# A two-layer decoder on one core: layer 0's contexts loaded turned, their norm moved into weights and evictions; layer 1's normed rows stored turned

## The chip, the cores and the metric

One core of a Trainium2 chip runs the whole program in one launch. The metric is the device time in microseconds (us) of one execution. Its engines are TensorE (PE: matrix products and, through products with an identity, transposes), VectorE (DVE), ScalarE (ACT), GpSimd (POOL) and SyncE (SP, which here only issues DMAs). Each engine works through its own queue in order; an instruction that waits holds up all behind it on that queue. PE writes its results to PSUM, and DVE or ACT must read ("evict") them before the PSUM bank can be used again.

## What is computed

A decoder of two layers on x (32 batches of 100 tokens, 256 wide, float32). Each layer has self-attention, cross-attention to contexts of 361 rows of 192, and a feed-forward part with experts. Two parts matter here.

Layer 0's cross-attention normalizes the contexts, then makes keys and values from them:

```
xn = layernorm(ctx, ln_x_g, ln_x_b)          # (32, 361, 192): mean and variance per row
ln = layernorm(layernorm(x), ln_l_g, ln_l_b) # (32, 100, 256)
q  = ln @ Wq.T
kv = concat([xn @ Wkv.T, ln @ Wlkv.T])       # 461 rows, 256 keys and 256 values
```

Keys and queries are normalized per head of 64, the scores masked, exponentials taken, and the weighted values projected and added to x.

Layer 1's feed-forward part takes the normed rows xn = layernorm(x). All rows go through one shared expert, silu(xn @ w1.T) @ w2.T, and each row also through two of eight experts with weights from a softmax.

## The kernel before

The program is unrolled and its stages follow each other. In each stage the program order of PE, DVE, ACT and POOL is the one written (`in_order`, L227); SP's order is written by hand only in the last two stages, elsewhere the framework sets it. PSUM has eight banks: two `sc` tiles of two banks each, and four `mm` tiles of one bank (`mm_tile`). A new `mm` tile takes a bank that has been read out.

**Layer 0's self-attention** (to about 290 us) is `heads_attention`: round s makes the scores of batch s+1, turns the weights of batch s (`turn_weights`, L390 on PE and L395 on ACT), makes values and sums. `fill(s, part)` is called at four places in a round and puts in work for the next stage: the first context loads, norms and turns.

**Layer 0's cross-attention** (about 290 to 760 us) works on one batch a round, at several depths at once. The loop over n (from L922) writes the order out. For a context, round n does: `context(n+6)`, the load of its rows (L552, L555); `context_normed(n+6, 0)`, mean and variance on DVE (L161, L162, L170) and the factor by a power on POOL (L174); `context_normed(n+5, 1)`, the centred and scaled rows `cn` on DVE (L183); `context_turned(n+4, 0)` and `(n+4, 1)`: transposes on PE (L574 for columns 0 to 127, L577 for the last 64, made twice, into both halves of the partitions) and evictions with gain and bias into cT by ACT (L583) and DVE (L587). Then `keys_values(n+3)`: eight products on PE (L720, L725; four tiles, two of 512 columns and two of 256), evicted by ACT (keys and values of the first 128 rows, keys of the last 105) and DVE (the rest), L733 to L737.

The rest of a round, in order: the square of the keys on ACT (`squares(n+2)`, L762), `keys_turned(n+1)` (PE L798, L806; kT by ACT L801; the queries qT by DVE L809), POOL's `divided(n, 1)` (L865) after DVE's reciprocal (L864), `output(n-1)` (PE L223 with x_wo, DVE L909), the sums of squares (L768) and the root on POOL (L772), `own_keys_values(n+3)` (PE L223 with x_wl into two tiles; keys by ACT L751, values by DVE L757), `turn_weights(n)` (PE L874, ACT L877), `keys_normed(n+2)` (L779, L780 on DVE, L782 on POOL), the keys and values above, `scores(n+1)` (L832 into `sc` tiles), `sums(n)` (L888), `exponentials(n+1)` (per head DVE L851 subtracts and masks, ACT L855 takes the exponential; after two heads ACT copies the sums out, L898), and `divided(n+1, 0)`. Every four rounds `latents_turned` adds eight transposes.

**Layer 1's cross-attention** ends at about 2835 us. Among its rounds `gating(g, part)` normalizes the rows of four batches (part 1, ACT L192), stores them to DRAM (`xn_dram`, L1589), turns them for the gate (part 2: transposes L210, evictions L131 and L133 into gT, one buffer, which lnT of the next group uses two units later) and sorts them to the experts.

**The shared expert** (about 2835 to 3025 us) loads blocks of 512 normed rows (`rows_of`, L2064), turns them (`rows_turned`: eight transposes L2077, evictions L131 and L133) and then makes, for every 256 rows and 128 hidden columns, L223 with the first weights, Silu on ACT (L2104) and the second product L2112. The routed experts follow to the end.

Of the kernel before, what the change touches and what calls it, by code (L numbers as in the profile page):

```python
# [10 lines left out]
F32 = mybir.dt.float32  # L11
# [7 lines left out]
P = 128  # L19
B, T, D = 32, 100, 256  # L20
S2, DC = 361, 192
G = 4
# [44 lines left out]
def kernel(ctx: ExitStack, tc: tile.TileContext, io: dict, out: bass.AP):  # L67
# [82 lines left out]
    def stats(src, n, np_=T, twice=False, tag="", half=None, got=None, shift=False):  # L150
# [7 lines left out]
        va = small.tile([P, G], F32, tag="va", name="va")  # L158
        rs = norms.tile([P, G], F32, tag="rs" + tag, name="rs")
        for i in range(n // 2 if half == 1 else 0, n // 2 if half == 0 else n):  # L160
# [374 lines left out]
    cbs, cns, cTs, lns, lnTs = {}, {}, {}, {}, {}  # L535

# [13 lines left out]
    def context(b):  # L550
        cb = cbuf[b % 2]
        nc.sync.dma_start(  # L552
            cb[:, 0:2, :], io["ctx"][b, 0:256].rearrange("(c p) d -> p c d", p=P)
        )
        nc.sync.dma_start(cb[:105, 2, :], io["ctx"][b, 256:S2])  # L555
        cbs[b] = cb

    def context_normed(b, part):
        if part == 0:
            cns[b] = stats(cbs[b], 3, P, tag="c")  # L560
        else:
            cn = early_ctx.tile([P, 3, DC], F32, tag="cn", name="cn")
            centered(cn, cbs.pop(b), 3, cns[b], P)
            cns[b] = cn

    def context_turned(b, c):

        if c == 0:
            cTs[b] = early_ctx.tile([P, 2, S2], F32, tag="cT", name="cT")
        cn, cT = cns[b], cTs[b]  # L570
        pt = mm_tile()
        for k, (k0, kn) in enumerate(CCH):
            if c == 0:
                nc.tensor.transpose(pt[:, k0 : k0 + kn], cn[:kn, k, 0:P], ident[:kn, :kn])  # L574
                continue
            for e in range(2):
                nc.tensor.matmul(  # L577
                    pt[64 * e : 64 * e + 64, k0 : k0 + kn], cn[:kn, k, P:DC],
                    ident[:kn, :kn], start=True, stop=True, tile_position=(0, 64 * e),
                )  # L580
        gain, bias = col("x0_xg", c), col("x0_xb", c)
        if c == 0:
            return lambda: nc.scalar.activation(  # L583
                cT[:, 0, :], pt[:, :S2], AF.Identity, bias=bias, scale=gain
            )
        cns.pop(b)
        return lambda: nc.vector.tensor_scalar(  # L587
            cT[:, 1, :], pt[:, :S2], gain, bias, ALU.mult, ALU.add
        )

    with tc.tile_pool(name="a0", bufs=2) as pool:
# [19 lines left out]
        def fill(s, part):  # L611
            for f, *args in {
                (B - 5, 0): ((context, 0), (context, 1)),
                (B - 3, 0): ((context_normed, 0, 0),),
                (B - 3, 2): ((latents, 0, 0),),
                (B - 2, 0): ((latents, 0, 1),),
                (B - 2, 2): ((context_normed, 0, 1),),
                (B - 1, 0): ((context_normed, 1, 0),),
                (B - 1, 1): ((latents, 0, 2),),
                (B - 1, 3): ((context_normed, 1, 1),),  # L620
            }.get((s, part), ()):
                f(*args)
            if s < B:
                return
            if part == 0:
                lnTs[0] = latents_turned(lns.pop(0))
            elif part < 3:
                context_turned(0, part - 1)()
            else:
                latents(1, 0)  # L630
                context(2)
                context_normed(2, 0)

# [53 lines left out]
    with tc.tile_pool(name="x0", bufs=2) as pool, tc.tile_pool(name="x0p", bufs=1) as fixed:  # L687
# [7 lines left out]
        for n in range(3):  # L695
# [15 lines left out]
        def keys_values(b, part):  # L711
# [18 lines left out]
            kvs.pop(b), cTs.pop(b)  # L730
            kb, vb = kbs[b], vbs[b]
            for n, copy in enumerate((nc.scalar.copy, nc.vector.tensor_copy)):
                copy(kb[:, n, :], ps[n][:, :D])  # L733
                copy(vb[:, n, :], ps[n][:, D:])
            kn = CCH[2][1]
            nc.scalar.copy(kb[:kn, 2, :], ps[2][:kn, :D])
            nc.vector.tensor_copy(vb[:kn, 2, :], ps[3][:kn, :D])  # L737

        def own_keys_values(b):

            lnT = lnTs[b // G]
            kb = kbs[b] = kbuf[b % 3]
            vb = vbs[b] = pool.tile([P, 4, D], F32, tag="vb", name="vb", bufs=4)
# [12 lines left out]
            )  # L756
            nc.vector.tensor_copy(vb[:T, 3, :], ps[:T, :D])  # L757

# [29 lines left out]
        def keys_turned(b, c):  # L788
# [20 lines left out]
            nc.vector.tensor_scalar(  # L809
                qT.rearrange("p c t -> p (c t)"), pt[:, : 2 * T], gains, None, ALU.mult  # L810
            )
# [106 lines left out]
        with in_order():  # L918


            for n in range(-3, B + 1):
                at(n + 6, context)  # L922
                at(n + 2, mask, 0)
                at(n + 2, squares)
# [8 lines left out]
                for k in range(4):  # L933
                    at(n, turn_weights, k)
                at(n + 5, context_normed, 1)
                if 0 <= n + 4 < B:
                    context_turned(n + 4, 0)()
                g = (n + 4) // G + 1
# [3 lines left out]
                if (n + 5) % G >= 1 and g + 1 < NG:  # L942
                    latents(g + 1, (n + 5) % G - 1)
                at(n + 6, context_normed, 0)
                at(n + 2, keys_normed)
# [590 lines left out]
    x_dram = dram.tile([NTOK, D], F32, name="x_dram")  # L1536
    xn_dram = dram.tile([NTOK, D], F32, name="xn_dram")
    acc_dram = dram.tile([NTOK + P, D], F32, name="acc_dram")
# [15 lines left out]
    )  # L1554
    gated = {}

    def largest(val, which, got=None):
# [24 lines left out]
    def gating(pool, g, part):  # L1582
# [4 lines left out]
        elif part == 1:  # L1587
            scaled(xs[g], xs[g], G, gated[g])
            nc.sync.dma_start(  # L1589
                xn_dram[g * GT : (g + 1) * GT, :].rearrange("(i t) d -> t i d", t=T), xs[g]  # L1590
            )
# [86 lines left out]
    with tc.tile_pool(name="x1", bufs=2) as pool, tc.tile_pool(name="x1p", bufs=1) as fixed:  # L1678
# [297 lines left out]
        with in_order():  # L1976
            for part in range(2):
                normed(0, part)
            lns[0] = turned(lns[0])
            qTs[0] = query_tile()  # L1980
            for m in range(8):
                queries(qTs[0], lns[0], m)
            keys(0, 0)
            keys(0, 1)
            for n in range(-2, NU):
                turn_of(n)
            for n in range(NU, NU + 4):
                sends(n)
            for part in range(3):
                finish(NG - 1, part)  # L1990
# [63 lines left out]
    with tc.tile_pool(name="f1s", bufs=2, side="right") as pool, in_order(SP):  # L2054
        xns_, xTs_, hTs, accs, held = {}, {}, {}, {}, {}
        pace = pool.tile([1, 1], F32, name="pace", bufs=1)
        NB = -(-NCH // 4)
        NHB = -(-NCH // 2)

        def rows_of(n):  # L2060

            cn = min(4, NCH - 4 * n)
            xn = pool.tile([P, 4, D], F32, tag="xn", name="xn")
            nc.sync.dma_start(  # L2064
                xn[:, :cn, :],
                xn_dram[512 * n : 512 * n + cn * P, :].rearrange("(c p) d -> p c d", p=P),
            )
            xns_[n] = xn

        def rows_turned(n):  # L2070
            cn = min(4, NCH - 4 * n)
            xn = xns_.pop(n)
            xT = pool.tile([P, 2, 512], F32, tag="xT", name="xT")
            for c in range(2):
                pt = mm_tile()
                for i in range(cn):
                    nc.tensor.transpose(  # L2077
                        pt[:, i * P : (i + 1) * P], xn[:, i, c * P : (c + 1) * P], ident
                    )
                evac(xT[:, c, : cn * P], pt[:, : cn * P])  # L2080
            xTs_[n] = xT
# [352 lines left out]
```

## Time and profile before

| | us |
|---|---|
| runs (3): median, lowest, highest | 3462.12, 3460.7, 3464.12 |
| profiled execution: its time | 3460.8 |
| profiled execution: its span | 3458.9 |

| busy in the span | us | share |
|---|---|---|
| PE, products | 3314.0 | 96% |
| PE, weight loads (beside the products) | 2237.8 | 65% |
| DVE | 1861.8 | 54% |
| ACT | 1632.0 | 47% |
| POOL | 1247.4 | 36% |

The profile is of one execution. A timeline line gives the start in us from the span's start, the length in us of that piece, the engine, the source line and operation, output and input tiles with their shapes, and how many instructions were merged; in brackets, how long the engine had been idle and what ended that. PE instructions are pipelined: what one costs is read from its start to the next one's start, since the length includes the time that the result takes to arrive. In a line of groups, the numbers behind the bar are the busy time in us, the mean length of one in ns, and the idle time before them with the releaser. The slice line has 40 digits, each the busy tenths of a fortieth of the span. "Granted clock" is the share of full speed that the throttle gave PE.

### The profile page before, as it was taken

Reading aid. Unit: us, or ns where it says so; the run is one execution under the profiler, and the core shown is the slowest. Engines: PE = TensorE matmul, PEld = TensorE weight load, DVE = VectorE, ACT = ScalarE, POOL = GpSimd, SP = SyncE. Lnnn points to the kernel's source line nnn. Section 1 sums busy time; section 2 is a strip of 40 time slices with the busy share of each in tenths; the row PEclk is TensorE's granted clock in tenths of the full one; section 3 lists DMA queues with packets and bytes.
Section 4 is the critical chain, followed back from the end, with each engine's and each line's share of the span. In section 5 each row is a group of like instructions: output and inputs, shape, how many; then the busy total and the mean of one; then the engine's idle time right before and its main releaser. Section 6 shows DMA issues by size and latency. Waiting matters only on the chain. (4 is left out here: it accounts for less than half of the span.)

```text
span 3458.9 us, 66312 instructions
## 1 busy us (share of the span) xinstructions
PE 3314.0 (96%) x25946; PEld 2237.8 (65%) x25946; DVE 1861.8 (54%) x5281; ACT 1632.0 (47%) x3597; POOL 1247.4 (36%) x932
## 2 busy tenths in 40 slices
PE   7999999998999989999999999999999989999997
PEld 5775666666666643333666666666666658899997
DVE  6777777758777657654446555555655542011111
ACT  4664666656444326665545455554555532211111
POOL 3445888864434331011323334333333332022221
PEclk9999999999999999999999999999999999999999
DMA  3001000001111110001000001000010012556665
GB/s 86 2 2 41 23 23 23 20 17 36 28 30 27 35 58 18 1 1 40 10 10 24 23 17 32 15 24 25 18 29 17 22 49 93 168 167 176 183 184 147
DMA packets 109073, 168.08 MB, mean 49 GB/s; under 512 B 14980, under 2 KB 89484, under 8 KB 108300
## 3 DMA queue, kind: packets, MB, share of 16 engines
q1 hardware_dynamic: 94094, 145.53, 13.8%
q0 software_dynamic: 12688, 15.36, 2.4%
q8 instruction: 207, 3.39, 0.4%
q10 hardware_dynamic: 1982, 2.95, 0.3%
q14 instruction: 102, 0.84, 0.1%
HBM read 138.26 MB, written 28.82 MB: 48 GB/s over the span
## 5 line engine op out<-in xcount | busy, mean ns | idle before, releaser
L1820 POOL TENSOR_TENSOR ex<-ex,rc 100x1444 f32<-100x1444 f32 x128 | 331.6, 2591 | 770.6 <-DVE rc L1819 526.7
L1811 ACT ACTIVATE ex<-s,nmx 100x361 f32<-100x361 f32 x512 | 303.1, 594 | 121.0 <-DVE nmx L1802 121.0
L378 POOL TENSOR_TENSOR s<-s,nmx 100x800 f32<-100x800 f32 x128 | 194.9, 1523 | 298.8 <-DVE nmx L377 219.0
L1385 ACT ACTIVATE h<-sc,cols 128x800 f32<-128x800 f32 x256 | 222.1, 923 | 102.9 <-PE sc L1379 101.4
L1802 DVE CUSTOM_DVE_ANT_0 s<-sc,mb 100x361 f32<-100x361 f32 x512 | 250.6, 528 | 7.5 <-PE sc L1795 7.5
L2283 POOL DMA_INDIRECT acc_dram<-y,xg x57 | 89.5, 1570 | 450.4 <-DVE y L2282 218.8
L2265 ACT ACTIVATE hgT<-sc 128x1024 f32<-128x1024 f32 x57 | 58.3, 1023 | 350.8 <-PE sc L223 350.8
L2282 DVE TENSOR_SCALAR y<-mm,gx 128x256 f32<-128x256 f32 x57 | 27.6, 484 | 347.8 <-PE mm L223 347.8
L223 PE MATMUL sc<-xgT,w1b 128*128 128x128 f32 x1824 | 213.1, 275 | 0.4 <-DMA w1b<-in_f_w 0.4
L223 PEld LDWEIGHTS sc<-xgT,w1b 128*128 128x128 f32 x1824 | 208.2, 192 | 0.7 <-DVE xgT L2250 0.6
L223 PE MATMUL mm<-wx,hgT 128*128 x912 | 206.1, 379 | 0.0
L1245 PE MATMUL mm<-xg,f_we 128*128 128x400 f32 x512 | 191.5, 516 | 14.1 <-DVE xg L1233 13.7
L1795 PE MATMUL sc<-kT,qT 64*100 64x361 f32 x1024 | 197.7, 463 | 0.0
L1767 PE MATMUL mm<-x_wa,cT 128*128 128x512 f32 (+1 forms) x512 | 188.8, 491 | 0.2
L223 PEld LDWEIGHTS mm<-wx,hgT 128*128 128x128 f32 x912 | 169.0, 190 | 20.6
L1737 PE MATMUL mm<-cT,x_wa 128*128 128x361 f32 x512 | 179.7, 470 | 1.1 <-ACT lnT L139 1.1
L1845 PEld LDWEIGHTS mm<-eT,vb 128*64 128x64 f32 (+1 forms) x3072 | 136.8, 137 | 67.3 <-issue 66.4
L1827 PE MATMUL mm<-ident,ex 100*128 100x100 f32 (+1 forms) x1536 | 165.5, 256 | 9.9 <-ACT kT L1749 5.3
L1834 ACT COPY eT<-mm 128x400 f32<-128x400 f32 (+1 forms) x256 | 125.7, 491 | 99.3 <-PE mm L1827 97.6
L174 POOL TENSOR_TENSOR rs<-va,neghalf 100x4 f32<-100x4 f32 (+1 forms) x96 | 95.6, 998 | 196.7 <-DVE va L170 100.3
L1845 PE MATMUL mm<-eT,vb 128*64 128x100 f32 (+1 forms) x3072 | 162.3, 254 | 0.0
L1827 PEld LDWEIGHTS mm<-ident,ex 100*128 100x128 f32 (+1 forms) x1536 | 142.4, 151 | 28.4 <-ACT kT L1749 7.0
(349 smaller groups left out, 7194.2 us busy)
## 6 DMA issues: line engine op xcount, KB each, us to landing
w1b<-in_f_w SPq DMA_DIRECT2D x57, 1024.0 KB
wb<-wt_dram SPq DMA_DIRECT2D x64, 200.0 KB
wx<-in_f_w SPq DMA_DIRECT2D x8, 1024.0 KB
xg<-sorted_dram SPq DMA_DIRECT2D x57, 132.5 KB
cb<-in_ctx SPq DMA_DIRECT2D x32, 192.0 KB
cT<-in_ctxT SPq DMA_DIRECT2D x32, 180.5 KB
cT<-in_ctxT SPq DMA_DIRECT2D x64, 90.2 KB
x<-in_x SPq DMA_DIRECT2D x8, 400.0 KB
```

The source lines that it names most:

```text
L223: nc.tensor.matmul(ps, lhsT[k], rhs[k], start=(k == 0), stop=(k == n - 1))
L378: nc.gpsimd.tensor_tensor(sm, sm, bc(nmx, 2, T), ALU.add)
L1245: nc.tensor.matmul(ps[:, :GT], f0_we[:, k, e * D + m * P : e * D + (m + 1) * P], xgs[E * g + e][:, k, :], start=(i > 0 and e == 2 * i and ...
L1385: nc.scalar.activation(h1, both[r2][:, :, :GT], AF.Tanh, bias=col("a1_b1", o))
L1737: nc.tensor.matmul(kTs[u][c][:, :S2], x1_wa[:, m * P : (m + 1) * P], cT[:, 0, :], start=True, stop=False,)
L1767: nc.tensor.matmul(ps[e][:kn, :n], cT[:, 0, at], x1_wa[:, 1024 + c0 : 1024 + c0 + n], start=True, stop=False,)
L1795: nc.tensor.matmul(ps[:T, e, :S2], qT[p0 : p0 + 64, m, tok], kT[p0 : p0 + 64, c, :], start=True, stop=True,)
L1802: nc.vector.tensor_tensor_reduce(s[:, e, :], ps[:T, e, :S2], mb, 1.0, 3.4e38, ALU.add, ALU.min, nmx[:, e : e + 1],)
L1811: nc.scalar.activation(ex[:, 2 * c + e, :], s[:, e, :], AF.Exp, bias=nmx[:, e : e + 1], scale=-1.0, accum_out=sm[:, 2 * c + e : 2 * c + e ...
L1820: nc.gpsimd.tensor_tensor(ex, ex, bc(rc, 2, S2), ALU.mult)
L1827: nc.tensor.transpose(pt[:kn, j * T : (j + 1) * T], ex[:, j, k0 : k0 + kn], ident[:T, :T])
L1845: nc.tensor.matmul(po[64 * e : 64 * e + 64, m * T : (m + 1) * T], vb[k][:kn, v0 + 64 * h : v0 + 64 * h + 64] if k < 2 else vb[2 + u % 2][: ...
```

## The change

Layer 0: (xn - mean) * r * g + b, times Wkv, is rewritten. The gain g goes into the rows of the weights, the mean is taken off by subtracting from each weight column its mean over the 192 rows, the row factor r is a scalar per row of the product, applied in the eviction, and the bias is a row b @ Wkv, added there too (`kv_bias`). So the raw contexts are loaded, already turned, from an array that layer 1 uses too (`ctxT`); the rows are still loaded, for the variance alone. The evictions of `keys_values` become six DVE instructions with three operands; qT and the own values go from DVE to ACT; the tile buffers `kb` go from three to two, cT from two to four, the factors `rs` from three to five. The weights are prepared in three rounds of layer 0's self-attention.

Layer 1: the normed rows are stored turned, from gT, so the shared expert loads them turned (`turned_rows`, three buffers) and makes no transposes; the first 512 are loaded at the end of the stage before, into a tile of their own.

```diff
+    def centered_weights(part):
+        if part == 0:
+            shift = early_ctx.tile([P, 2, P], F32, tag="cT", name="shift", bufs=4)
+            for c in range(2):
+                nc.vector.tensor_copy(shift[:, c, :], col("x0_xb", c).to_broadcast([P, P]))
+            ps = mm_tile()
+            project(ps, [shift[:, 0, :], shift[:64, 1, :]], [x0_wa, x0_wb[:64]])
+            nc.scalar.copy(kv_bias.rearrange("p c d -> p (c d)"), ps)
+        elif part == 1:
+            for w, c in ((x0_wa, 0), (x0_wb, 1)):
+                nc.vector.tensor_scalar(w, w, col("x0_xg", c), None, ALU.mult)
+        else:
+            mean = early_ctx.tile([P, P], F32, tag="cT", name="mean", bufs=4)
+            nc.gpsimd.memset(mean, 1.0 / DC)
+            ps = mm_tile()
+            project(ps, [mean, mean[:64]], [x0_wa, x0_wb[:64]])
+            for w in (x0_wa, x0_wb):
+                nc.vector.tensor_tensor(w, w, ps, ALU.subtract)
...
-    def context_normed(b, part):
...
-    def context_turned(b, c):
...
+    def context_turned(b):
+        cT = cTs[b] = early_ctx.tile([P, 2, S2], F32, tag="cT", name="cT", bufs=4)
+        nc.sync.dma_start(cT[:, 0, :], io["ctxT"][b, 0:P])
+        for e in range(2):
+            nc.sync.dma_start(cT[64 * e : 64 * e + 64, 1, :], io["ctxT"][b, P:DC])
+    def context_scale(b):
+        crs[b] = stats(crs[b], 3, P, tag="c")[1]
...
         def fill(s, part):
+                (B - 16, 1): ((centered_weights, 0),),
+                (B - 15, 1): ((centered_weights, 1),),
+                (B - 14, 1): ((centered_weights, 2),),
...
         def keys_values(b, part):
-            for n, copy in enumerate((nc.scalar.copy, nc.vector.tensor_copy)):
-                copy(kb[:, n, :], ps[n][:, :D])
-                copy(vb[:, n, :], ps[n][:, D:])
-            kn = CCH[2][1]
-            nc.scalar.copy(kb[:kn, 2, :], ps[2][:kn, :D])
-            nc.vector.tensor_copy(vb[:kn, 2, :], ps[3][:kn, :D])
+            rs = crs.pop(b)
+            for n, (_, kn) in enumerate(CCH):
+                for c, dst in enumerate((kbs[b], vbs[b])):
+                    src = ps[n][:kn, c * D : c * D + D] if n < 2 else ps[n + c][:kn, :D]
+                    nc.vector.scalar_tensor_tensor(
+                        dst[:kn, n, :], src, rs[:kn, n : n + 1], kv_bias[:kn, c, :],
+                        ALU.mult, ALU.add,
+                    )
...
         def own_keys_values(b):
-            nc.vector.tensor_copy(vb[:T, 3, :], ps[:T, :D])
+            nc.scalar.copy(vb[:T, 3, :], ps[:T, :D])
...
         def keys_turned(b, c):
-            nc.vector.tensor_scalar(
-                qT.rearrange("p c t -> p (c t)"), pt[:, : 2 * T], gains, None, ALU.mult
+            nc.scalar.activation(
+                qT.rearrange("p c t -> p (c t)"), pt[:, : 2 * T], AF.Identity, scale=gains
...
             for n in range(-3, B + 1):
                 at(n + 6, context)
+                at(n + 6, context_turned)
...
-                at(n + 5, context_normed, 1)
-                if 0 <= n + 4 < B:
-                    context_turned(n + 4, 0)()
...
-                at(n + 6, context_normed, 0)
+                at(n + 6, context_scale)
...
-                out_ = context_turned(n + 4, 1) if 0 <= n + 4 < B else None
...
-                if out_:
-                    out_()
...
         elif part == 1:
             scaled(xs[g], xs[g], G, gated[g])
-            nc.sync.dma_start(
-                xn_dram[g * GT : (g + 1) * GT, :].rearrange("(i t) d -> t i d", t=T), xs[g]
-            )
         elif part == 2:
             transposed(gT, xs[g], tiles=mm_tile)
+            nc.sync.dma_start(xT_dram[:, :, g * GT : (g + 1) * GT], gT)
...
             for n in range(-2, NU):
                 turn_of(n)
+            nc.sync.dma_start(xT_first, xT_dram[:, :, :512])
...
-        def rows_of(n):
...
-        def rows_turned(n):
...
+        def turned_rows(n):
+            n0, n1 = 512 * n, min(512 * n + 512, NTOK)
+            xT = pool.tile([P, 2, 512], F32, tag="xT", name="xT", bufs=3)
+            nc.sync.dma_start(xT[:, :, : n1 - n0], xT_dram[:, :, n0:n1])
...
-        rows_of(0)
+        for n in range(1, 3):
+            turned_rows(n)
...
-        rows_of(1)
-        rows_turned(0)
...
-                if m == 4 and h % 2 == 1 and h // 2 + 1 < NB:
-                    rows_turned(h // 2 + 1)
-                    if h // 2 + 2 < NB:
-                        rows_of(h // 2 + 2)
+                if m == 4 and h % 2 == 0 and h >= 2 and h // 2 + 2 < NB:
+                    turned_rows(h // 2 + 2)
```

More of the change, by code (lines that the diff above doesn't have):

```diff
@@ L158, in stats @@
         va = small.tile([P, G], F32, tag="va", name="va")
-        rs = norms.tile([P, G], F32, tag="rs" + tag, name="rs")
+        rs = norms.tile(
+            [P, G], F32, tag="rs" + tag, name="rs", **(dict(bufs=5) if tag == "c" else {})
+        )
         for i in range(n // 2 if half == 1 else 0, n // 2 if half == 0 else n):
@@ L534 @@
         cbuf.append(cb)
-    cbs, cns, cTs, lns, lnTs = {}, {}, {}, {}, {}
+    crs, cTs, lns, lnTs = {}, {}, {}, {}
+    kv_bias = w1.tile([P, 2, D], F32, name="kv_bias")
+    def centered_weights(part):
[16 more added lines that the diff above has]
+                nc.vector.tensor_tensor(w, w, ps, ALU.subtract)
     def latents(g, part):
@@ L555, in context @@
         nc.sync.dma_start(cb[:105, 2, :], io["ctx"][b, 256:S2])
-        cbs[b] = cb
-    def context_normed(b, part):
[L559 to L564, printed above, removed]
-    def context_turned(b, c):
[L568 to L579, printed above, removed]
-                )
[L581 to L589, printed above, removed]
+        crs[b] = cb
+    def context_turned(b):
[5 more added lines that the diff above has]
+        crs[b] = stats(crs[b], 3, P, tag="c")[1]
     with tc.tile_pool(name="a0", bufs=2) as pool:
@@ L612, in fill @@
             for f, *args in {
+                (B - 16, 1): ((centered_weights, 0),),
+                (B - 15, 1): ((centered_weights, 1),),
+                (B - 14, 1): ((centered_weights, 2),),
                 (B - 5, 0): ((context, 0), (context, 1)),
-                (B - 3, 0): ((context_normed, 0, 0),),
+                (B - 4, 0): ((context_turned, 0), (context_turned, 1)),
+                (B - 3, 0): ((context_scale, 0),),
                 (B - 3, 2): ((latents, 0, 0),),
                 (B - 2, 0): ((latents, 0, 1),),
-                (B - 2, 2): ((context_normed, 0, 1),),
-                (B - 1, 0): ((context_normed, 1, 0),),
+                (B - 1, 0): ((context_scale, 1),),
                 (B - 1, 1): ((latents, 0, 2),),
-                (B - 1, 3): ((context_normed, 1, 1),),
             }.get((s, part), ()):
@@ L626, in fill @@
                 lnTs[0] = latents_turned(lns.pop(0))
-            elif part < 3:
-                context_turned(0, part - 1)()
-            else:
+            elif part == 3:
                 latents(1, 0)
                 context(2)
-                context_normed(2, 0)
+                context_turned(2)
+                context_scale(2)
         fill.steps = 0
@@ L694 @@
             mbuf.append(mb)
-        for n in range(3):
+        for n in range(2):
             kb = fixed.tile([P, 5, D], F32, tag=f"kb{n}", name=f"kb{n}")
@@ L730, in keys_values @@
             kvs.pop(b), cTs.pop(b)
-            kb, vb = kbs[b], vbs[b]
-            for n, copy in enumerate((nc.scalar.copy, nc.vector.tensor_copy)):
-                copy(kb[:, n, :], ps[n][:, :D])
-                copy(vb[:, n, :], ps[n][:, D:])
-            kn = CCH[2][1]
-            nc.scalar.copy(kb[:kn, 2, :], ps[2][:kn, :D])
-            nc.vector.tensor_copy(vb[:kn, 2, :], ps[3][:kn, :D])
+            rs = crs.pop(b)
[5 more added lines that the diff above has]
+                        ALU.mult, ALU.add,
+                    )
         def own_keys_values(b):
             lnT = lnTs[b // G]
-            kb = kbs[b] = kbuf[b % 3]
+            kb = kbs[b] = kbuf[b % 2]
             vb = vbs[b] = pool.tile([P, 4, D], F32, tag="vb", name="vb", bufs=4)
@@ L1536 @@
     x_dram = dram.tile([NTOK, D], F32, name="x_dram")
-    xn_dram = dram.tile([NTOK, D], F32, name="xn_dram")
+    xT_dram = dram.tile([P, 2, NTOK], F32, name="xT_dram")
     acc_dram = dram.tile([NTOK + P, D], F32, name="acc_dram")
@@ L1555 @@
     gated = {}
+    xT_first = w5.tile([P, 2, 512], F32, name="xT_first")
     def largest(val, which, got=None):
@@ L1588, in gating @@
             scaled(xs[g], xs[g], G, gated[g])
-            nc.sync.dma_start(
-                xn_dram[g * GT : (g + 1) * GT, :].rearrange("(i t) d -> t i d", t=T), xs[g]
-            )
         elif part == 2:
@@ L2054 @@
     with tc.tile_pool(name="f1s", bufs=2, side="right") as pool, in_order(SP):
-        xns_, xTs_, hTs, accs, held = {}, {}, {}, {}, {}
+        xTs_, hTs, accs, held = {0: xT_first}, {}, {}, {}
         pace = pool.tile([1, 1], F32, name="pace", bufs=1)
@@ L2058 @@
         NHB = -(-NCH // 2)
-        def rows_of(n):
[L2062 to L2068, printed above, removed]
-        def rows_turned(n):
[L2071 to L2080, printed above, removed]
+        def turned_rows(n):
+            n0, n1 = 512 * n, min(512 * n + 512, NTOK)
+            xT = pool.tile([P, 2, 512], F32, tag="xT", name="xT", bufs=3)
+            nc.sync.dma_start(xT[:, :, : n1 - n0], xT_dram[:, :, n0:n1])
             xTs_[n] = xT
```

## The prediction

> **What bounds the kernel now.** I read first the page's busy shares and slices, then the timelines of the four stretches that the change touches, then the groups by form for prices. The chain that ended last has three pieces, 6 us at the end, and says nothing here.
>
> ```profile
> PE   7999999998999989999999999999999989999997
> ```
>
> TensorE (PE) is busy in every slice. So a stretch is worth what PE can no longer do or must wait for in it. Layer 0's cross-attention loop runs from about 290 to 760 us. One round, by the timeline (start, length, engine, line):
>
> ```profile
> 504.01 0.64 DVE L851 CUSTOM_DVE_ANT_0 s<-sc,mb 100x461 f32<-100x461 f32 x1
> ...
> 508.00 0.17 DVE L864 RECIPROCAL rc<-sm 100x2 f32<-100x2 f32 x1 [0.34 <-ACT ex L855]
> 508.09 0.41 DVE L809 TENSOR_SCALAR qT<-mm,gains 128x200 f32<-128x200 f32 x1
> 508.71 2.74 PE L223 MATMUL mm<-x_wl,lnT 128*100 128x512 f32 x8
> 508.92 0.42 DVE L909 TENSOR_TENSOR x<-x,mm 100x256 f32<-100x256 f32 x1 [0.42 <-PE mm L223]
> 511.30 1.56 PE L874 MATMUL mm<-ident,ex 100*128 100x100 f32 x16
> 512.70 0.48 PE L574 MATMUL mm<-ident,cn 128*128 128x128 f32 x3
> 513.01 2.76 PE L720 MATMUL mm<-x_wa,cT 128*128 128x512 f32 x8
> 515.70 1.56 PE L725 MATMUL mm<-x_wb,cT 64*128 64x512 f32 x8
> 516.91 0.42 DVE L733 COPY kb<-mm 128x256 f32<-128x256 f32 x1 [0.81 <-PE mm L725]
> 518.09 0.64 DVE L851 CUSTOM_DVE_ANT_0 s<-sc,mb 100x461 f32<-100x461 f32 x1
> ```
>
> The round is 14.08 us (504.01 to 518.09) and PE is full in it. But a ring of waits is just as long. Call D the first L851. L851 (four times), four exponentials and the second reciprocal L864 take 3.99. L809 follows on VectorE (DVE), and its end at 508.50 frees a PSUM bank. With four `mm` tiles, the own-keys product (L223, x_wl) can use that one: PE starts it at D+4.70. Then PE needs 2.59 to L874, 1.40 to L574, 0.31 to L720, 2.69 to L725 and 1.21 to DVE's first eviction; 1.18 later is the next D. The sum is 4.70+2.59+1.40+0.31+2.69+1.21+1.18 = 14.08. PE and the ring are level, so work taken off PE pays only if the ring gets shorter too.
>
> **Part 1, the loop.** Removed from PE: L574 (0.31 to the next start) and L577 (from 506.10 to 506.82, where L798 begins, 0.72), together 1.03, which would leave PE 13.05. Only L574 lies on the ring. From DVE go the three `cn` instructions, L587, L757 and L809; from ScalarE (ACT) the L583 and three key/value copies; ACT gets the own-value copy and qT. None of these moved ones lies on the ring, except what L809 did: see below.
>
> Added: all six key/value evictions are now on DVE, ahead of L851 on the same queue, and behind L851 wait the exponentials. The nearest row for a scalar_tensor_tensor out of PSUM with 256 columns is L1884:
>
> ```profile
> 2833.42 1.66 DVE L1884 SCALAR_TENSOR_TENSOR x<-mm,valid,x 100x256 f32<-100x256 f32 x4 [5.96 <-PE mm L1877]
> ```
>
> Four in 1.66 with 0.48 for one make a step of 0.393. Six end 5x0.393+0.48 = 2.45 after the first start, and the next instruction starts some 0.08 before that: 2.37 instead of 1.18, **+1.19 on the ring**. (The bounds: as copies, step 0.335, 2.0; as a two-scalar op like L587, 0.57 for 361 columns, so 0.43 a step, 2.6.)
>
> Then the bank. At the own-keys product the four tiles are the two key transposes (read by ACT's L801, behind a 1.26 square), the query transpose (its reader is now on ACT behind L801 too) and the output tile, read by L909 on DVE. L909 is first, right after the reciprocal. The four exponentials end 0.22 earlier, since ACT's oT copy between them no longer waits for PE's sums (506.32, though ACT was free at 506.10): reciprocal at D+3.77, L909 at +3.85, end +4.27, and with 0.15 of handover (o ends 287.28, L432 starts 287.43) PE at D+4.42. New round: 4.42+2.59+1.40+2.69+1.21+2.37 = **14.68**, +0.60. PE would idle 1.6 of it. The eT copies on ACT, four tiles later, end just as L720 wants their banks (D+8.40 against +8.43), so I add nothing, up to 0.3. POOL's kn and weights end over 0.4 ahead of their readers. Rounds with evictions: n = 0 to 28, 29 x 0.60 = **+17**. Bounds by the eviction step and the eT copies: 29x0.2 = +6 and 29x0.95 = +28.
>
> The cT loads (three per context, q1) are issued three rounds before use and share a DMA load of a tenth: nothing; one round's lateness at the start would be 2 us. The five `rs` buffers and two `kb` add no wait that I find: own keys write kb after kn of the round before ended (some 5 us of slack).
>
> **The clock.** [...] In this trace:
>
> ```profile
> 308.40 1.02 PE L798 MATMUL mm<-ident,kn 128*128 128x128 f32 x8 [2.38 <-POOL kn L782]
> ...
> 309.48 4.39 PE L223 MATMUL mm<-x_wl,lnT 128*100 128x512 f32 x8
> ```
>
> After 2.38 us of idling the same eight products take 4.39 instead of 2.74, 1.65 more. A gap of 1.65 before L390 at 845.29 cost nothing visible. The new round has about 0.8 and 0.9 of idling, 0.9 apart. I take one round in ten to lose 1.65: 29x0.1x1.65 = **+5** (0 if never; 29x0.25x1.65 = +12 if one in four). [...]
>
> **Part 2, the weights (attention of layer 0, rounds 16 to 18).** PE is 95% busy there.
>
> ```profile
> 252.75 1.03 PE L223 MATMUL mm<-a_w,xT 128*100 128x256 f32 x4
> ...
> 253.56 1.52 POOL L378 TENSOR_TENSOR s<-s,nmx 100x800 f32<-100x800 f32 x1 [2.65 <-ACT eT L395]
> ```
>
> The new products stand where PE starts L223 at 252.75. L720 makes 1536 columns in 2.69, so two products of 512 take 1.8. Step one needs two broadcasts by DVE, behind an L366 that runs from 253.34 to 254.32: ready at about 254.7, PE waits 2.0, and works 1.8. Step two is two DVE multiplications of 512 columns (the L148 row's 0.69 for 400 columns out of PSUM, each): half hidden, 0.6. Step three needs a POOL memset behind L378 (ends 255.08): PE waits 2.5, works 1.8, and DVE, which waits for the product with L377 queued behind it, subtracts. 3.8+0.6+4.3 = 8.7; PE has 0.3 of idling a round to give back: **+8** (3.6 if only the products count, 10.5 with all).
>
> **Part 3, the start of the loop.** L574 and L577 (about 1.0 each) and an 0.85 wait go twice before the first D; the first evictions take 1.2 more: **-1** (-3 to 0).
>
> **Part 4, the shared expert.**
>
> ```profile
> 2841.86 1.94 PE L2077 MATMUL mm<-ident,xn 128*128 128x128 f32 x8 [8.04 <-DMA xn<-xn_dram]
> 2842.23 2.09 ACT L192 ACTIVATE x<-x,sh,rs 100x256 f32<-100x256 f32 x4 [9.44 <-DMA x_dram<-x]
> ...
> 2866.13 1.04 PE L2077 MATMUL mm<-ident,xn 128*128 128x128 f32 x8
> ```
>
> The eight transposes of a block cost 0.87 to the next start (2867.00); five blocks and a quarter give 4.6. PE's 8.04 wait for the rows looks like a larger prize, but ACT waits at the same place for another DMA, the x rows' store, then scales (2.09) and loads its table (1.28) ahead of the first Silu. PE can run three products early and then waits for that Silu, about 1.3 earlier than now, and cold afterwards, which takes back about 1: 0.4 gained. **-5** (-8 to -3). The gT store (400 KB, as the xn store was) ends long before lnT, two units of 9 us later, reuses its buffer: nothing; 1 us a group, 7 in all, if it did not.
>
> **Sum**, against the profiled execution's own 3460.8 (span 3458.9; the median of the runs is 1.3 higher): 17+5+8-1-5 = +24, **3485 us**. With the bounds of the parts, 3459 to 3508 if all go one way; the likely part 3470 to 3500.
>
> **Rivals.**
> *PE sets the round (faster).* If the own-keys product got a bank by D+2.8 instead of +4.42, the ring would be no longer than PE's 13.05: 29 x -1.03 = -30, no clock term: -30+8-1-5 = -28, 3433. For it: PE is busy 100.00 of 100.00 in the windows from 400 to 600. Against: the four readers named above, none of which ends before D+4.2.
> *The worse bank.* If that product gets the tile that L801 reads (its first copy ended 509.56, D+5.55, so +5.3 now), the round is 1.1 longer again: +32 more, 3517.
> *Nothing gained or lost.* If the evictions overlap PE's scores better than by my step, the ring stays at 14.08: 8-1-5, 3463.
> *It does not do what it says.* The first turned rows might be loaded behind the sorted_dram write, as the row load is now (SP held until 2836.3). PE would start at 2842 as now, ACT still bounds it: no change to part 4 worth more than 1.
>
> **Chances.** Forecast 0.58, faster 0.20 (3433), worse bank 0.12, nothing 0.10. The range runs from 3435 to 3508, leaving out the worse bank and a part of the fast case, under 0.2. A difference of 0.2% (7 us) is what can be told from no change: faster 0.21, within 0.11, slower 0.68.
>
> **What would show it.** Right: L851 follows the first eviction by 2.3 to 2.6; rounds of 14.5 to 15 in which PE's x_wl waits for L909; no L574, L577 or L2077; slow PE stretches in a few rounds; PE waiting 2 us for DVE and for POOL in two attention rounds. Wrong: rounds near 13, or x_wl starting straight after x_wo; x_wl waiting for L801 would be the worse bank. The weak points are which tile frees the bank, and how often the clock drops.

## The result, and the profile after

| | before | after |
|---|---|---|
| median of five executions, us | 3460.70 (3458.57 to 3464.12) | 3476.02 (3474.99 to 3484.45) |
| ratio to before | | 1.0049, 95% interval 1.0034 to 1.0064 |
| profiled execution, us (span, mean granted clock) | 3460.8 (3458.9, 0.986) | 3484.45 (3482.7, 0.982) |

The change makes the kernel 15 us slower. The profiled execution of after is its slowest; the other four took 3474.99 to 3478.77 at a granted clock of 0.985 or 0.986. So the traces differ by 23.8 us where the medians differ by 15.3, and what lies between them has to be explained too.

In the 40 slices TensorE (PE) is still busy everywhere:

```profile
PE   7998999988999988999999999999999989999997
```

The page says no more than before. I set the starts of VectorE's (DVE) unchanged instructions in the two traces side by side and read where the difference grows:

| stage (times of before) | difference at its end | grown in it |
|---|---|---|
| self-attention to round 15 (to 161 us) | +0.3 | +0.3 |
| rounds 16 to 18 (to 202) | +15.1 | **+14.9** |
| rest, and start of the loop (first mask-add at 319.79) | +11.8 | **-3.3** |
| loop of layer 0 (last round's mask-add at 756.05) | +26.8 | **+15.0** |
| after the loop (to 832) | +32.0 | **+5.2** |
| layer 1 up to the shared expert (to 2837) | +31.2 | -0.8 |
| shared expert (to 3007) | +23.2 | **-8.0** |
| to the end | +23.8 | +0.6 |

One round of the loop, by the timeline of after (start, length, engine, line; the line numbers of this function are one or two higher than in before):

```profile
508.47 0.63 DVE L852 CUSTOM_DVE_ANT_0 s<-sc,mb 100x461 f32<-100x461 f32 x1
...
512.14 0.17 DVE L865 RECIPROCAL rc<-sm 100x2 f32<-100x2 f32 x1 [1.29 <-ACT ex L856]
512.23 0.40 DVE L910 TENSOR_TENSOR x<-x,mm 100x256 f32<-100x256 f32 x1
...
512.68 2.82 PE L225 MATMUL mm<-x_wl,lnT 128*100 128x512 f32 x8 [0.75 <-DVE x L910]
...
515.35 1.57 PE L875 MATMUL mm<-ident,ex 100*128 100x100 f32 x16
...
516.75 2.77 PE L720 MATMUL mm<-x_wa,cT 128*128 128x512 f32 x8
...
519.45 1.56 PE L725 MATMUL mm<-x_wb,cT 64*128 64x512 f32 x8
...
520.61 0.48 DVE L735 SCALAR_TENSOR_TENSOR kb<-mm,rs,kv_bias 128x256 f32<-128x256 f32 x1 [1.57 <-PE mm L725]
...
522.97 0.63 DVE L852 CUSTOM_DVE_ANT_0 s<-sc,mb 100x461 f32<-100x461 f32 x1
```

The round is 14.50 us where it was 14.08. PE now idles 0.75 ahead of x_wl, and what ends it is L910. PE's waits from 331 to 690 us, added up (total, times, longest), name the same reader once in each of the 24 plain rounds (all but the first and the last six):

```profile
PE mm L225 <- DVE x L910: 17.9, 24, 0.8
```

In the loop's first round, where no L910 comes ahead of x_wl, PE waits for another reader:

```profile
336.64 1.35 PE L225 MATMUL mm<-x_wl,lnT 128*100 128x256 f32 x4 [2.63 <-ACT kT L802]
337.78 2.91 PE L875 MATMUL mm<-ident,ex 100*128 100x100 f32 x16
```

From L875 to the next product (340.49) it takes 2.71 there, not 1.40: the granted clock is 0.50 from 337.4 to 340.8 us.

In the three attention rounds the added products stand behind two waits:

```profile
168.99 1.10 PE L225 MATMUL mm<-x_wa,shift 128*128 128x512 f32 x2 [1.70 <-issue]
170.01 2.01 PE L225 MATMUL mm<-x_wb,shift 64*128 64x512 f32 x2
...
192.47 0.20 POOL L554 MEMSET mean<- 128x128 f32 x1
192.73 1.13 PE L225 MATMUL mm<-x_wa,mean 128*128 128x512 f32 x2 [2.08 <-POOL mean L554]
193.79 1.89 PE L225 MATMUL mm<-x_wb,mean 64*128 64x512 f32 x2
```

The first of each pair takes 1.1, the second 1.9 to 2.0 for the same number of columns: the granted clock is 1.00 from 168 to 170.1 us and 0.50 from there to 176.9, 1.00 from 192 to 194.0 and 0.50 from there to 200.8. The table of wider windows shows it too (window, its length, then busy time of PE, PEld, DVE, ACT and POOL with counts; the third number from the end is PE's granted clock):

```profile
168.00:178.00 10.00, 9.01 (x74) 5.03 (x78) 2.33 (x5) 3.27 (x6) 3.97 (x4) 0.66 0.14 39
178.00:190.00 12.00, 11.77 (x137) 8.55 (x130) 9.80 (x23) 6.30 (x13) 5.08 (x5) 1.00 0.01 1
190.00:202.00 12.00, 9.91 (x85) 5.46 (x83) 4.37 (x6) 4.02 (x9) 3.71 (x6) 0.72 0.11 31
```

0.34 of 10 us and 0.28 of 12 are 3.4 us lost in each: two stretches of 6.8 us at half clock.

And the start of the shared expert:

```profile
2864.61 1.66 DVE L1879 SCALAR_TENSOR_TENSOR x<-mm,valid,x 100x256 f32<-100x256 f32 x4 [5.96 <-PE mm L1872]
2864.84 2.75 PE L225 MATMUL mm<-xT_first,w 128*128 128x256 f32 x12
2865.16 1.52 SPq L1882 DMA_DIRECT2D x_dram<-x  x4
...
2867.65 1.41 SPq L2160 DMA_DIRECT2D sorted_dram<-empty  x1
...
2870.04 2.08 ACT L194 ACTIVATE x<-x,sh,rs 100x256 f32<-100x256 f32 x4 [6.06 <-POOL sh L178]
...
2873.43 0.94 ACT L2084 ACTIVATE hT<-mm 128x256 f32<-128x256 f32 x3
```

PE has no transposes and no 8 us wait ahead of its first product. But ScalarE's (ACT) scale, too, starts 5.4 us behind the residual (8.8 before), and no longer waits for a DMA: SP's queue has the x_dram stores ahead of the sorted_dram write, where before they stood behind it. The lines of before:

```profile
2836.32 0.36 SPq L2180 DMA_DIRECT2D sorted_dram<-empty  x1
2836.98 0.39 SPq L2064 DMA_DIRECT2D xn<-xn_dram  x1
2837.42 1.94 SPq L1887 DMA_DIRECT2D x_dram<-x  x4
...
2846.10 0.38 ACT L2104 ACTIVATE hT<-mm 128x256 f32<-128x256 f32 x1
```

### The profile page after: what moved, and what is told of

Its sections match the earlier page's. It is cut to its first block, busy times and chain, and to the rows that moved or that the text cites. A ratio compares the mean times of both kernels' runs of the same rounds, so it can differ in the third digit from the quotient of the medians.

```text
span 3482.7 us, 65280 instructions
## 1 busy us (share of the span) xinstructions
PE 3308.1 (95%) x25424; PEld 2214.1 (64%) x25424; DVE 1827.5 (52%) x5184; ACT 1601.9 (46%) x3527; POOL 1247.5 (36%) x932
## 5 line engine op out<-in xcount | busy, mean ns | idle before, releaser
L856 ACT ACTIVATE ex<-s,nmx 100x461 f32<-100x461 f32 x128 | 86.0, 674 | 184.9 <-DVE nmx L852 184.9
```

## The experiments

My theory, from these traces: the loop's ring is closed by L910's bank and lengthened by the six evictions; the attention rounds pay for two products, two waits and, in some executions, two half-clock stretches; the shared expert's part adds up by itself. The rival in each place is that the work of an engine sets the time, so that banks and waits could move without changing it.

**ffn_alone.** The kernel before with the layer 1 part only.

```diff
-            nc.sync.dma_start(xn_dram[...], xs[g])
+            nc.sync.dma_start(xT_dram[:, :, g * GT : (g + 1) * GT], gT)
...
-        rows_of(0)
+        for n in range(1, 3):
+            turned_rows(n)
...
-        rows_turned(0)
```

> The kernel before with only the layer 1 part of the change (turned rows stored, loaded by the shared expert). Theory (the parts add up): the two profiled executions stand 31.2 us apart before this part and 23.4 after it, so it gives 7.8 us by itself: 3453 us, with PE's first product of the shared expert 4 us earlier and 3.6 us more saved over the later blocks. Rival 1 (my own step of the prediction, 5 us): 3456. Rival 2 (the gain belongs to the slower loop ahead of it, which gives its transfers time): no change, 3461.

Measured: 3453.02 us, 0.9977 of before (0.9968 to 0.9986). The layer 1 part by itself is a gain of 7.9 us, as much as the table's -8.0 in the whole change; so layer 0's part costs 23 by the medians.

**prep_early.** The operands of the added products one attention round earlier.

```diff
+                (B - 17, 1): ((centered_weights, -1),),
                 (B - 16, 1): ((centered_weights, 0),),
...
+        if part == -1:
+            prep["shift"] = early_ctx.tile([P, 2, P], F32, tag="cT", name="shift", bufs=4)
...
+            nc.gpsimd.memset(prep["mean"], 1.0 / DC)
```

> The changed kernel, but the two broadcasts of shift and the memset of mean are made one attention round earlier (round 15), with the products where they are. Theory (PE's waits for DVE and POOL cost 1.7 and 2.1 us, and the idle time is also what brings two half-clock stretches in the profiled execution, about 3.4 us each): neither wait is there, no half clock between 160 and 200 us, the three rounds cost some 4 us instead of 14.9; 3472 us against 3476 for the median of the changed kernel, and 7 us more against an execution that had the slow stretches. Rival (PE would have waited in those rounds anyway, so the waits only move to the next reader): 3476, and the three rounds still cost 8 or more.

Measured: 3471.54 us, 1.0035 (1.0023 to 1.0047). The three rounds cost 4.65 us instead of 14.9. No wait over 0.2 stands ahead of the four products, and in this execution the windows that had 0.66 and 0.72 are at full clock:

```profile
168.00:178.00 10.00, 9.77 (x106) 6.32 (x105) 5.72 (x9) 5.78 (x13) 3.13 (x4) 1.00 0.14 39
...
190.00:202.00 12.00, 10.93 (x162) 7.80 (x153) 8.41 (x15) 6.89 (x13) 4.75 (x7) 1.00 0.07 23
```

**bank_early.** The first key transposes, with their copy on ACT, between the two pairs of exponentials.

```diff
-                at(n + 1, keys_turned, 0)
...
                 at(n, sums_out)
+                at(n + 2, keys_turned, 0)
                 at(n + 1, exponentials, 1)
```

> The changed kernel with one order changed in layer 0's loop: the first key transposes, with ScalarE's copy of them, stand between the two pairs of exponentials of the round before instead of behind them. The own-keys product then gets the bank that this copy frees. Nothing is removed. Theory (a ring of waits closed by the bank that L910 frees sets the round of 14.50): PE's x_wl starts right behind x_wo, 5.8 us after the first eviction instead of 6.57, the round is 13.75 and the loop 21 us shorter: 3455 us, under the kernel before. Rival (the six evictions or the work of an engine set the round, whichever bank is free): round 14.4 to 14.5, 3476; as the exponentials of the second pair come half a us later, it could be 14.9 and 3488.

Measured: 3458.81 us, 0.9995 (0.9986 to 1.0004): 17 us under the changed kernel. The round is 13.65:

```profile
500.53 0.54 ACT L802 COPY kT<-mm 128x461 f32<-128x461 f32 x1
...
500.68 1.11 PE L225 MATMUL mm<-x_wo,oT 128*100 128x256 f32 x4
...
501.62 2.74 PE L225 MATMUL mm<-x_wl,lnT 128*100 128x512 f32 x8
...
502.43 0.17 DVE L865 RECIPROCAL rc<-sm 100x2 f32<-100x2 f32 x1 [1.73 <-ACT ex L856]
502.52 0.40 DVE L910 TENSOR_TENSOR x<-x,mm 100x256 f32<-100x256 f32 x1
```

x_wl starts straight behind x_wo and 0.9 us *ahead* of L910, for which it waited before. No engine does less; the bank was the bound. The 24 plain rounds give 24 x 0.85 = 20.4. The loop as a whole is 18.6 shorter in the traces: the four rounds near the end that also prepare the next attention fall by 1.0 together (15.3 to 15.5, where they were 15.5 to 15.8), and the first round and the last two are 2.9 longer.

**bank_early_before.** The same two lines in the kernel before.

> The same order changed in the kernel before. Theory (there PE's own work, 14.08 a round, is as long as the ring, so a shorter ring buys nothing): rounds of 14.0 to 14.1, 3461 us, within 5. Rival (the ring alone set 14.08 and PE's work was shorter): rounds of 13.4, 3441.

Measured: 3467.22 us, 1.0017 (1.0008 to 1.0026). A bank that is free earlier bought nothing there: the round is 14.24, x_wl starts 4.70 behind L851 as it did, straight behind x_wo. I had not counted the loss of 0.16 a round: the second pair of exponentials comes later, and with it GpSimd's (POOL) weights, which L874 reads; it takes 1.56 to the next product instead of 1.40. So in the kernel before PE's own 14.08 was the bound, as the prediction had it.

**values_on_scalar.** The three value evictions on ACT.

```diff
+                    if c == 1:
+                        nc.scalar.activation(
+                            dst[:kn, n, :], src, AF.Identity, scale=rs[:kn, n : n + 1]
+                        )
+                        continue
                     nc.vector.scalar_tensor_tensor(
```

> The changed kernel with the three value evictions on ScalarE, as scaled copies; the bias of the values is left out of the computation. VectorE keeps the three key evictions. Theory (the ring is closed by L910's bank and runs through the six evictions): L852 follows the first eviction by 1.3 instead of 2.36, and the 24 plain rounds of the loop shorten by 1.1 each, from 14.50 to 13.4: 3449 us. Rival 1 (the moved bank alone made the rounds longer): 14.50, 3476. Rival 2 (ScalarE, which would now do the copies, is late for the exponentials): 14 or more, 3464.

Measured: 3457.23 us, 0.9994 (0.9984 to 1.0003), in the direction of the theory but with only half its size: rounds of 13.91, not 13.4.

```profile
490.12 1.27 DVE L740 SCALAR_TENSOR_TENSOR kb<-mm,rs,kv_bias 128x256 f32<-128x256 f32 x3 [1.31 <-PE mm L725]
...
491.35 0.64 DVE L857 CUSTOM_DVE_ANT_0 s<-sc,mb 100x461 f32<-100x461 f32 x1
...
494.57 1.03 PE L225 MATMUL mm<-x_wo,oT 128*100 128x256 f32 x4
...
495.64 0.42 DVE L915 TENSOR_TENSOR x<-x,mm 100x256 f32<-100x256 f32 x1
```

The mask-add does follow the first eviction by 1.23. But the residual add (L915 here) now starts with the end of x_wo (495.60) and not behind the reciprocal: PE's own sums, transposes and x_wo are the next link, and they take back half a us. A ring shortened in one place is held by the next one.

**interleaved.** bank_early, and the evictions spread between the four mask-adds.

```diff
+                evicted(n + 3, (2, 0), (2, 1), (0, 0))
...
                 at(n + 1, exponentials, 0)
+                evicted(n + 3, (0, 1))
...
+                exponentials(n + 1, 1, lambda: evicted(n + 3, (1, 0)))
                 at(n + 1, divided, 0)
+                evicted(n + 3, (1, 1))
```

(A pair names the chunk and whether it is its keys, 0, or its values, 1; each is one of the six evictions.)

> The changed kernel with bank_early's order, and the six evictions spread between the four L852: first the two of the third chunk (each frees a bank by itself) and the first keys, then two L852, and one eviction behind each of the later ones; PE's output product stands ahead of the query transposes. All six stay on VectorE and nothing is left out. Theory (both halves of the ring, the evictions ahead of L852 and the bank, are then shorter than PE's own 13.05): 13.05 to 13.2 a round, 0.5 under bank_early's 13.65, and 3445 us, under the kernel before. Rival (VectorE's or GpSimd's own work sets some 13.6 a round): 3458, as bank_early.

Measured: 3446.33 us, 0.9959 (0.9946 to 0.9973). Rounds of 13.16: 0.1 over the 13.05 that the prediction gave PE.

**interleaved_prep.** interleaved with prep_early's edit, both diffs as above.

> interleaved with prep_early's edit as well. Theory (the two act in different stages and add up): 4.5 us less than interleaved, 3440 us, about 0.6% under the kernel before. Rival (they share a cause): as interleaved.

Measured: 3436.50 us, 0.9927 (0.9914 to 0.9941): 24 us under the kernel before, and 5 under the sum of the two gains (each of these medians stands in executions that spread over 8 or 9). A round of it:

```profile
506.57 0.64 DVE L872 CUSTOM_DVE_ANT_0 s<-sc,mb 100x461 f32<-100x461 f32 x1 [0.31 <-PE sc L851]
...
507.69 0.48 DVE L749 SCALAR_TENSOR_TENSOR vb<-mm,rs,kv_bias 128x256 f32<-128x256 f32 x1
...
508.64 0.48 DVE L749 SCALAR_TENSOR_TENSOR kb<-mm,rs,kv_bias 128x256 f32<-128x256 f32 x1
...
509.62 1.03 PE L225 MATMUL mm<-x_wo,oT 128*100 128x256 f32 x4
...
510.66 2.74 PE L225 MATMUL mm<-x_wl,lnT 128*100 128x512 f32 x8
```

Now VectorE waits for PE and not PE for VectorE: the mask-add waits 0.31 for the scores, and PE goes from x_wo through the query transposes to x_wl without a wait.

**queries_on_vector.** The query transposes' eviction back on DVE.

```diff
-            nc.scalar.activation(
-                qT.rearrange("p c t -> p (c t)"), pt[:, : 2 * T], AF.Identity, scale=gains
+            nc.vector.tensor_scalar(
+                qT.rearrange("p c t -> p (c t)"), pt[:, : 2 * T], gains, None, ALU.mult
             )
```

> The changed kernel with one part undone: VectorE again evicts the query transposes (a two-scalar op of 0.41 between the second reciprocal and L910). Theory (any reader behind the second reciprocal frees the bank, so it does not matter which): this eviction frees the own-keys bank as early as L910 does now, x_wl starts 4.2 us after the first L852 as now, rounds of 14.5, 3476 us within 4. Rival 1 (the move to ScalarE was the harm, by the worse bank): rounds of 14.1, 3465. Rival 2 (it was a gain): 14.8, 3484.

Measured: 3477.92 us, 1.0053 (1.0037 to 1.0068), rounds of 14.51: it does not matter which of these two readers behind the reciprocal frees the bank (PE's x_wl waits for L810 here). Its trace shows something else by chance. Its attention rounds are the changed kernel's, with the same waits:

```profile
168.58 1.10 PE L225 MATMUL mm<-x_wa,shift 128*128 128x512 f32 x2 [1.70 <-issue]
169.60 1.12 PE L225 MATMUL mm<-x_wb,shift 64*128 64x512 f32 x2
...
189.11 1.24 PE L225 MATMUL mm<-x_wa,mean 128*128 128x512 f32 x2 [2.09 <-POOL mean L554]
190.28 2.07 PE L225 MATMUL mm<-x_wb,mean 64*128 64x512 f32 x2
```

Behind the same 1.70 the granted clock is 1.00 here (168 to 178 us), behind the same 2.1 it is 0.72 (190 to 202). The three rounds cost 11.6 us: 14.9 less one stretch of 3.4.

**rows_written_aside.** The kernel before, with the sorted_dram write on ACT's queue.

```diff
-        nc.sync.dma_start(sorted_dram[E * RG :, :], empty)
+        nc.scalar.dma_start(sorted_dram[E * RG :, :], empty)
```

> The kernel before with one write (sorted_dram from empty, L2180) issued from ScalarE's queue instead of SP's; the shared expert still loads rows and turns them. In the kernel before this write holds SP's queue until 2836.32, and the row load and the four x_dram stores behind it go out at 2836.98 and 2837.42, though DVE has the first of these rows at 2833.9. In the changed kernel the stores stand ahead of the write, and ScalarE's scale, which waited for them, starts 3.3 us sooner. Theory (the order of SP's queue, not the loaded turned rows, gives what the shared expert's start gained over my step): stores at 2834 to 2835, ScalarE's scale near 2839, first Silu 3 us sooner than 2846.10, 3457.5 us against 3460.7. Rival 1 (PE's wait for the rows and the transposes behind it is the bound, as the turned load removes it): PE's transposes start sooner too, near 2838, and it is the same 3 us, but the Silu waits for PE and not for ScalarE's table load. Rival 2 (neither): 3460.7; ScalarE, which must issue the write itself, could be late instead, 3463.

Measured: 3458.44 us against 3459.99 for the kernel before, measured beside it, 0.9996 (0.9987 to 1.0005): the interval holds both 3 us and nothing, so the time alone decides nothing. The stage does. At the residual this execution is 2.35 us behind that of before (2833.42), and at the first Silu 1.05 ahead (2846.10):

```profile
2835.77 1.66 DVE L1884 SCALAR_TENSOR_TENSOR x<-mm,valid,x 100x256 f32<-100x256 f32 x4 [5.96 <-PE mm L1877]
...
2836.74 1.82 SPq L1887 DMA_DIRECT2D x_dram<-x  x4
...
2841.20 2.08 ACT L192 ACTIVATE x<-x,sh,rs 100x256 f32<-100x256 f32 x4 [6.06 <-POOL sh L176]
...
2845.05 0.38 ACT L2104 ACTIVATE hT<-mm 128x256 f32<-128x256 f32 x1
```

The stores go out 1.0 behind the residual (4.0 before), the scale starts as soon as POOL has the factors, and the Silu follows the table load: 3.4 us without a single row that is loaded turned. PE's transposes came sooner too (2840.70), but the Silu waited for ACT's scale and table, as the theory says.

## Why the prediction was right, and where it was wrong

**The loop, forecast +17, measured +15.0: right, link by link.** From the mask-add: x_wl after 4.21 (4.42 forecast), then 2.67 (2.59), 1.40 (1.40), 2.70 (2.69), 1.16 (1.21) and 2.36 (2.37), 14.50 against 14.68. The term that is off is the first: L910 ends 4.16 behind the mask-add, not 4.27, and PE starts 0.05 later, not 0.15. With 0.42 for 0.60 the 24 plain rounds give 10.1; the rest I did not foresee: the first round is 2.1 longer, the four that prepare the next attention 2.1 together, the last two 0.7. In the first round x_wl waits for L802, the bank that the rival "the worse bank" named. In the plain rounds the bank is the one I named, and the step of the eviction is 0.39 as the L1884 row said. The rival in which PE sets the round failed for the reason given, and interleaved showed that its floor is real.

**The clock, forecast +5 in the loop: near in size by luck, wrong in place.** The loop's 24 plain rounds have no half-clock stretch: each has a wait of some 0.75 (24 add up to 17.9, the longest 0.8), and the granted clock is 1.00 from 345 to 690 us. Its first round has one, behind a wait of 2.63; both are part of that round's 2.1. Two longer ones came in the attention rounds, behind waits that the prediction had written down (2.0 and 2.5 forecast, 1.70 and 2.08 measured) without asking what they do to the clock. They cost the profiled execution 6.8 us. Behind the same 1.70 in queries_on_vector the clock stayed at 1.00; what decides that, no run shows.

**The weights, forecast +8: right.** Without the clock the three rounds cost 14.9 - 6.8 = 8.1 in the changed kernel and 11.6 - 3.4 = 8.2 in queries_on_vector. With the operands early they cost 4.65, so the two waits are 3.5 of it. Each pair of products takes some 2.1, not 1.8, and the two waits in the trace of after are 3.8 long, not 4.5, so the two errors offset each other.

**The start of the loop, forecast -1, measured -3.3: about right without the clock.** Both traces have half-clock stretches there, and not the same ones. Windows of before, then of after:

```profile
272.00:290.00 18.00, 14.68 (x139) 10.97 (x138) 13.07 (x34) 7.93 (x17) 5.36 (x6) 0.81 0.12 32
290.00:320.00 30.00, 27.02 (x131) 14.65 (x129) 22.06 (x74) 10.68 (x20) 16.12 (x10) 0.94 0.26 77
```

```profile
284.00:302.00 18.00, 14.15 (x162) 10.18 (x155) 13.49 (x40) 9.45 (x20) 6.66 (x9) 1.00 0.11 19
302.00:331.60 29.60, 25.07 (x100) 13.48 (x99) 19.35 (x64) 7.37 (x12) 17.00 (x11) 0.88 0.38 111
```

By these shares before loses some 5.2 us to the clock (18 x 0.19 and 30 x 0.06), after some 3.5 (29.6 x 0.12, in and behind a wait of 3.91 for GpSimd). That is 1.7 of the 3.3, and the rest, an estimate, is -1.6. At 276.90 in before and 292.02 in after PE waits 1.52 for the same copy; only in before does a half-clock stretch follow (0.50 from 279 to 285 us; in after 1.00 from 284 to 302).

**After the loop, not in the forecast, +5.2 in the traces.** It is the clock, as far as the traces go. The 50 us from 760 in after have a granted clock of 0.83, those from 733 in before 0.93. Behind the loop the difference grows in three steps of 2.1, 1.6 and 1.1 us, and each stands where the clock of after is low: 0.50 from 788 to 798 us, 0.57 from 815 to 819 and from 856 to 860. Before has 1.00 from 780 to 860. queries_on_vector, with the same code there, lost only 0.7. No run was made that changes the clock there alone.

**The shared expert, forecast -5, measured -8.0 (-7.9 by itself).** The transposes gave what I counted: five steps of 0.87 to 0.88, 4.4. The step that failed is the 0.4 for the start. ACT does still bound it, but I took the x_dram store that ACT waits for as fixed. It was not: the load of the rows and the write that held SP's queue stood ahead of it, and after the change neither does. rows_written_aside gave 3.4 us with that order alone; 4.4 and 3.4 are 7.8. The 1 us taken back for a cold PE stood on no row of before. In after the four products L2092, behind a wait of 6.26, do take 2.08 (four such products take 1.03 in rows_written_aside), at a granted clock of 0.52 from 2873 to 2877 us; but before has 0.57 from 2842 to 2846, too.

**The sum.** 3485 against 3484.45 for the profiled execution is closer than its terms, and that is luck: the loop was put 2 too high and the gain of the shared expert 3 too small, against a clock that took some 5 more than I gave it (6.8 + 5.2 - 1.7, where I gave 5). That execution is also the slowest of the five; the median rose by 15.3, where +24 was forecast. The terms without these three pieces of the clock, the loop's own stretch still in them, are 15.0 + 8.1 - 1.6 - 7.9 = 13.6. How the clock ran in the other executions stands in no trace.

## What to carry to other kernels

Before work is taken off a full engine, follow the ring of waits through the buffers: if it is as long as the engine's own work, the work taken away only turns into a wait, and what was added on the ring comes on top. The remedy was not less work but order: free the bank between two exponentials, and put evictions into the gaps of the instructions that others wait for (30 us under the changed kernel by the medians, 14 under the kernel before). Of an added step, prepare the operands a stage early, and look at what stands ahead of each DMA in its queue, for it moves too.

## What the runs showed of the hardware that I had not expected

- The two half-clock stretches of the attention rounds of after lasted 6.8 us each (0.50 from 170.1 to 176.9 and from 194.0 to 200.8 us) and cost 3.4 each, since PE is busy in all of both. The same waits brought one in one execution and not in the next: from 168 to 178 and from 190 to 202 us the granted clock is 0.66 and 0.72 in after, 1.00 and 0.72 in queries_on_vector. Without the waits, in prep_early and before, it is 1.00 in both.
- The last `o` of that attention on VectorE (o<-mm,rc) starts at 298.04, 298.50 and 296.87 us in after, interleaved and bank_early, and at 294.37 and 294.40 in values_on_scalar and queries_on_vector, all five with the same code up to there; with prep_early's edit it starts at 288.26 and 288.23 (prep_early, interleaved_prep). An estimate from these times, at 3.4 us a stretch: two such stretches in the first three, one in the next two.
- In after, the half-clock stretches from 160 us to the loop's first round start at 170.1, 194.0, 316.9 and 337.4 us, in or behind waits of 1.70, 2.08, 3.91 and 2.63. A wait of 1.52 that ends at 292.02 has none behind it. No run tests which waits bring one.
- Two stretches are 6.8 of the 8.4 us that separate the profiled execution of after from its median; that the other executions lack them is read from their times and granted clocks alone.
- A bank freed by VectorE was taken by PE 0.05 us after the end of the reading instruction (L910 ends at 512.63 us in after, x_wl starts at 512.68).
